# Adding the token stream to layer 0's mixed inputs: an accumulating DMA over both channel chunks in place of GpSimd's additions

## The chip, the cores and the metric

The kernel runs on one core of a Trainium2 chip. The metric is the device time of the whole program in microseconds; the figure quoted for the kernel before is the median of three runs. Five engines work side by side and meet through semaphores: TensorE (PE, with its weight loads shown as PEld), VectorE (DVE), ScalarE (ACT), GpSimd (POOL) and SyncE (SP). Transfers are issued from the queues of SP, ACT and POOL.

## The reference, cut to what matters

Two layers are computed on a stream of 8 x 512 tokens with 256 channels. In each layer the stream is normalised, a token mixer and a mixture of experts both read it, and both outputs are added to it. Layer 0's mixer is a bidirectional linear recurrence (RWKV style), its experts are 8 with the best 2 chosen; layer 1 has two attentions and 16 experts with a shared one.

The change lies in the front of layer 0's mixer, in the lines that make its five mixed inputs:

```
dx = xc - x                                  # xc: a 3-tap convolution along the tokens
xxx = x + dx * maa_x
t5 = tanh(xxx @ maa_w1).reshape(B, T, 5, 32)
m = einsum('btfc,fcd->fbtd', t5, maa_w2)
xw = x + dx * (maa_w + m[0])
xk = x + dx * (maa_k + m[1])
xv = x + dx * (maa_v + m[2])
xr = x + dx * (maa_r + m[3])
xg = x + dx * (maa_g + m[4])
r, k, v, g = xr @ Wr, xk @ Wk, xv @ Wv, silu(xg @ Wg)
w = time_decay + tanh(xw @ decay_w1) @ decay_w2
...
S = exp(wt)[..., None] * S + kt[..., None] * vt[..., None, :]    # the scan, forwards and backwards
```

The change is about who adds the leading `x` in the five lines from `xw` to `xg`.

## The kernel before, in words

**Layout.** A sequence (one of B = 8, index `b`) is kept transposed: channels on the 128 partitions, in NC = 2 chunks `c`, and T = 512 tokens along the row. `xnT` (L711) holds the normalised stream of one sequence with two columns of padding at each side; `xT[c]` are its inner 512 columns. There is one `xnT` buffer, so the next sequence's loading (the memsets L749 and L750 on GpSimd, the load L751 on SP) waits until the last reader of the present one is done.

**The order of the work.** The kernel is written as Python generators, each of which issues some instructions and then yields. `Turns.turn()` (L155) runs every live generator once; the order of the calls is the order of the instructions on PE, DVE, ACT and SP, whose order is pinned (L35, L373). GpSimd's order is not pinned: a scheduler sets it when the program is built. An engine works through its own list strictly in order.

In the main stage `scans` (L887) drives the turns. It goes through 128 units (b, c, vg), four turns each: a product of 128x1024 (L901), two scans forwards and backwards (L910, L914) in each of two turns, a second product (L923); PE sums the results two units later (L929). So one sequence is 64 turns. In each turn the other generators add a piece: `experts` (L592) works off 39 chunks of 256 token slots, 12 turns a chunk (L615 gate and up, L655 down); `ending` closes a chunk of channels; and `projections(b + 1)` (L672) prepares the next sequence while the present one is scanned.

`projections` has three generators, run one after the other for b >= 1 (L897): `inputs`, `values`, `decays`. For b = 0 they run beside the first normalisations (L1010 to L1018), before any scan, and `first` is true. Counting their yields gives 11 turns for `inputs`, 12 for `values` and 22 for `decays`: 45 of the 64.

**The lines of the change.** `mixed(*fs)` (L722) makes mixed inputs for the projections named by `fs`. It is called with (2, 1) in `values` for xv and xk, with (0, 3) in `decays` for xw and xr, and with (4) late in `decays` for xg. For each chunk `c` it issues the small matmuls on PE (L732, L734), yields, has VectorE write `(m + maa) * dx` (L739) and has GpSimd add `xT[c]` in place (L742). After both chunks it yields twice and returns the tiles, and the caller's matmuls come next (L697 for v, k, r and g; L815 for dw). One sequence has ten such additions, 128x512 fp32 each; eight sequences have 80.

The tiles come from `mix` (L688): tag `xf`, four buffers of 128x512. For b = 0 those of `decays` and the two `near` tiles take the `held` buffers instead.

**Other GpSimd work of the main stage.** It issues the experts' indirect gathers (L567 weights `wgu` and `wdn`, L577 tokens `xs`), stores the experts' results (L665), and multiplies `z` by `g` (L987), 16 times in all. `entry` (L273), which starts layer 1 on a sequence, gathers two expert rows per token into `y0` (L284 to L290) and adds them up (L298); in layer 0's last part `y0` and `cT` use the `xf` buffers as well (L1029).

Of the kernel before, what the change touches and what calls it, by code (L numbers as in the profile page):

```python
# [26 lines left out]
F32 = mybir.dt.float32  # L27
I32 = mybir.dt.int32
AF = mybir.ActivationFunctionType
ALU = mybir.AluOpType  # L30
# [6 lines left out]
P = 128  # L37
B, T, D = 8, 512, 256
NC = D // P
NT = T // P  # L40
H = 16
HD = 16
PAD = 2
# [122 lines left out]
def two_layers(ctx: ExitStack, tc: tile.TileContext, a: dict, out: bass.AP):  # L166
    nc = tc.nc
    vec_e, act_e, pool_e, pe = nc.vector, nc.scalar, nc.gpsimd, nc.tensor
# [8 lines left out]
    def held(i, shape, name):  # L177
        return hold.tile(shape, F32, tag=f"held{i}", name=name)
# [18 lines left out]
    def V(name, c):  # L197
        return vecs[:, VEC[name], c : c + 1]
# [9 lines left out]
    outs = stream.tile([NSLOT, D], F32, name="outs")  # L208
    slot = [const.tile([P, NTT], I32, name=f"slot{i}", tag=f"slot{i}") for i in range(2)]
# [63 lines left out]
    def entry(b):  # L273

        if b >= 3:
            yield from until("out", b - 3)
        bank, temp = place_of["bank"], place_of["temp"]
        acc = held(b % 3, [P, NT, D], f"acc{b}")
        nc.sync.dma_start(acc, tokens(after[b]))
        ahead = 2 if b else NT  # L280
        for t0 in range(0, NT, ahead):
            ys = []
            for t in range(t0, t0 + ahead):
                y = temp([P, 2, D], "y0", f"y0_{b}_{t}", ahead)  # L284
                n = b * NT + t
                for i in range(2):
                    pool_e.indirect_dma_start(
                        out=y[:, i, :], out_offset=None, in_=outs,
                        in_offset=bass.IndirectOffsetOnAxis(ap=slot[i][:, n : n + 1], axis=0),
                    )  # L290
                ys.append((t, n, y))
            yield
            yield
            if b == 0:
                yield from until("scans over")
            for t, n, y in ys:
                for i in range(2):
                    vec_e.scalar_tensor_tensor(  # L298
                        acc[:, t, :], y[:, i, :], wslot[i][:, n : n + 1], acc[:, t, :],
                        ALU.mult, ALU.add,  # L300
                    )
        yield
        x = held(3 + b % 3, [P, NT, D], f"x1_{b}")
        yield from layer_norm(x, acc, f"b{b}")
        yield
        if b >= 2:
            yield from until("ffn", b - 2)
        pss = transposed(bank, x, f"x_{b}")
        yield
        xT = held(6 + b % 2, [P, NC, T], f"xT_{b}")  # L310
        for c in range(NC):
            act_e.copy(xT[:, c, :], pss[c])
        own[b] = acc, x, xT
        done.add(("x", b))
        yield

        ps = bank(f"lg_{b}")
        for t in range(NT):
            for c in range(NC):
                pe.matmul(  # L320
                    ps[:, t * E1 : (t + 1) * E1], xT[:, c, t * P : (t + 1) * P], rtw[:, c, :],
                    start=c == 0, stop=c == NC - 1,
                )
        yield


        def rt(n, tag):
            return small.tile([P, NT, n], F32, tag=tag, name=f"{tag}_{b}", bufs=1)

        s, sb, sel = rt(E1, "rs"), rt(E1, "rsb"), rt(E1, "rsel")  # L330
        gsel, gs = rt(G1, "rg"), rt(G1, "rgs")
        act_e.activation(s.rearrange("p n e -> p (n e)"), ps[:, : NT * E1], AF.Tanh, scale=0.5)
        yield
        vec_e.tensor_scalar(s, s, 0.5, 0.5, ALU.mult, ALU.add)
        vec_e.tensor_tensor(sb, s, bc(cbias, 1, NT), ALU.add)

        def groups(x):
            return x.rearrange("p n (g e) -> p (n g) e", g=G1)

        chosen(groups(sel), groups(sb), E1 // G1, 2, C["tri4"], temp, f"g{b}")  # L340
        yield
        vec_e.tensor_tensor(sel, sel, sb, ALU.mult)
        vec_e.tensor_reduce(gs.rearrange("p n g -> p (n g)"), groups(sel), AX.X, ALU.add)
        chosen(gsel, gs, G1, 2, C["tri4"], temp, f"h{b}")
        flat = gsel.rearrange("p n g -> p (n g)")
        vec_e.tensor_tensor(groups(sb), groups(sb), bc(flat, 2, E1 // G1), ALU.mult)
        vec_e.tensor_scalar(gsel, gsel, FMAX, FMAX, ALU.mult, ALU.subtract)
        vec_e.tensor_tensor(groups(sb), groups(sb), bc(flat, 2, E1 // G1), ALU.add)
        for t in range(0, NT, 2):
            yield  # L350
            chosen(sel[:, t : t + 2, :], sb[:, t : t + 2, :], E1, 4, C["tri16"], temp, f"i{b}{t}")
        yield
        vec_e.tensor_tensor(sel, sel, s, ALU.mult)
        tot = small.tile([P, NT], F32, tag="rtot", name=f"rtot_{b}")
        vec_e.tensor_reduce(tot, sel, AX.X, ALU.add)
        vec_e.tensor_scalar(tot, tot, 1e-20, None, ALU.add)
        vec_e.reciprocal(tot, tot)
        vec_e.tensor_tensor(sel, sel, bc(tot, 2, E1), ALU.mult)
        yield
        ps = bank(f"cT_{b}")  # L360
        for t in range(NT):
            pe.transpose(ps[:E1, t * P : (t + 1) * P], sel[:, t, :], ident)
        yield
        cT = temp([E1, T], "cT", f"cT_{b}")
        act_e.copy(cT, ps[:E1, :])
        cd = shares_at.tile([E1, T], F32, tag="cd", name=f"cd_{b}")
        act_e.dma_start(cd, cT)
        own[b] += (cd,)
        done.add(("entry", b))


    with ExitStack() as l0:
        l0.enter_context(tc.manual_schedule(engines=PINNED))  # L373
        keep = l0.enter_context(tc.tile_pool(name="keep0", bufs=1))
        rw = l0.enter_context(tc.tile_pool(name="rw", bufs=1))
# [296 lines left out]
        def projections(b):  # L672


            first = b == 0
# [10 lines left out]
                return ps_gu.tile([P, T], F32, tag="gu", name=f"{name}_{b}") if first else bank(name)  # L686

            def mix(name, i, other=False):  # L688
                if other and first:
                    return held(i, [P, T], f"{name}_{b}")  # L690
                return rw.tile([P, T], F32, tag="xf", name=f"{name}_{b}", bufs=4)

            def project(w, xs, co, name, bank=bank):

# [16 lines left out]
            xnT = rw.tile([P, NC, T + 2 * PAD], F32, tag="xnT", name=f"xnT_{b}")  # L711
            xT = [xnT[:, c, PAD : PAD + T] for c in range(NC)]
            dx = big("dx", 1)
            dxs = [dx[:, c, :] for c in range(NC)]
            t5a = rw.tile([P, T], F32, tag="t5a", name=f"t5a_{b}")
            th = rw.tile([96, T], F32, tag="th", name=f"th_{b}")
# [4 lines left out]

            def mixed(*fs, other=False):  # L722

                xs = {f: [] for f in fs}
                for c in range(NC):
                    pss = []
                    for f in fs:
                        ps = (other_bank if other else bank)(f"m{f}{c}")
                        cols = slice(c * P, (c + 1) * P)
                        if f < 4:  # L730
                            rows = slice(32 * f, 32 * f + 32)
                            pe.matmul(ps, m2a[rows, cols], t5a[rows, :], start=True, stop=True)  # L732
                        else:
                            pe.matmul(ps, m2b[64:, cols], t5b, start=True, stop=True)  # L734
                        pss.append(ps)
                    yield
                    for f, ps in zip(fs, pss):
                        t = mix(f"xf{f}{c}", 2 * c + (f != fs[0]), other)
                        vec_e.scalar_tensor_tensor(  # L739
                            t, ps, V("maa_" + "wkvrg"[f], c), dxs[c], ALU.add, ALU.mult  # L740
                        )
                        pool_e.tensor_tensor(t, t, xT[c], ALU.add)  # L742
                        xs[f].append(t)
                yield
                yield
                return [xs[f] for f in fs]

            def inputs():
                pool_e.memset(xnT[:, :, 0:PAD], 0.0)  # L749
# [11 lines left out]
                    yield  # L761
                for _ in range(0 if first else 1):
                    yield
                xxx = []
                for c in range(NC):
                    t = mix(f"xxx{c}", c)
                    vec_e.scalar_tensor_tensor(t, dxs[c], V("maa_x", c), xT[c], ALU.mult, ALU.add)
                    xxx.append(t)
                for _ in range(1 if first else 2):
                    yield  # L770
                both = ((t5a, 0, 0, P), (t5b, P, 64, 96))
                pss = []
                for _, lo, r0, r1 in both:
                    ps = bank(f"t5{lo}")
# [32 lines left out]
            def decays():  # L807
# [5 lines left out]
                ps = other_bank("dw")  # L813
# [22 lines left out]
                vec_e.scalar_tensor_tensor(q, d, 1.0, q, ALU.add, ALU.mult)  # L836
                yield

                near = [mix(f"near{c}", 4 + c, True) for c in range(NC)]
                for c in range(NC):  # L840
                    act_e.activation(near[c], q[:, c, :T], AF.Ln, scale=-1.0)
                for c in range(NC):
# [177 lines left out]
        def begin():  # L1020
# [6 lines left out]
            act_e.dma_start(cbias, a["correction_bias"].to_broadcast([P, E1]))  # L1027

            tag_of = {  # L1029
                "y0": ("xf", 4), "gt4": ("t5a", 1), "eq4": ("th", 1), "gt16": ("dx", 1),  # L1030
                "eq16": ("xnT", 1), "cT": ("xf", 4),
            }
            place_of["bank"] = lambda name: ps_gu.tile([P, T], F32, tag="gu", name=name)
            place_of["temp"] = lambda shape, tag, name, bufs=1: rw.tile(
# [509 lines left out]
```

## Time and profile before

| What | Value |
|---|---|
| median of 3 runs | 2727.75 us (2727.06 to 2733.11) |
| the profiled execution | 2728.59 us, span 2726.8 us |
| PE, DVE busy | 2362.4 us (87%), 2157.0 us (79%) |
| ACT, POOL busy | 888.3 us (33%), 477.5 us (18%) |
| GpSimd's additions, L742 | 80 of 128x512, 113.3 us busy by the page |
| first scan product (L901) starts at | 97.9 us |
| last scan product (L923) starts at | 1422.5 us |

The span is the time of the profiled execution by its own records; the device time of that execution is 1.8 us longer. The page's second part cuts the span in 40 slices. Slices 3 to 21 are the main stage, in which DVE stands at 8 or 9 tenths throughout and PE mostly as well; the second half is layer 1, in which PE leads. In a group line the columns are the source line, the engine, the operation, output and inputs with shapes, the count, busy time and mean duration of one, and the idle time of the engine just before them with what ended it.

### The profile page before, as it was taken

The page shows a single profiled execution, that of the slowest core. Times are in us where ns is not written, and L with a number is a line of the kernel's source. Part 1 is how long each engine was busy: PE and PEld are TensorE (multiplying, and loading weights), DVE is VectorE, ACT ScalarE, POOL GpSimd, SP SyncE. Part 2 cuts the span into 40 slices and gives each one's busy share as a digit, 9 for nine tenths or more (in the row PEclk, how much of TensorE's full clock was granted, in tenths as well). Part 3 has the DMA queues.
Part 4 walks back from the last instruction along what each step waited for, and adds up shares of the span by engine and source line. Part 5 has one row for each costly group of instructions (what it writes and reads, how often), then busy time and mean ns, then how long its engine had stood idle before and what let it go on. Part 6 is the DMA issues. An engine that isn't in the chain of part 4 may idle for free.

```text
span 2726.8 us, 32763 instructions
## 1 busy us (share of the span) xinstructions
PE 2362.4 (87%) x11900; PEld 1412.8 (52%) x11900; DVE 2157.0 (79%) x3063; ACT 888.3 (33%) x1687; POOL 477.5 (18%) x441
## 2 busy tenths in 40 slices
PE   6699898988989889898826899999989989898996
PEld 4355555555556545555503445555555555555554
DVE  7799999899999989989985755656576675756666
ACT  1233232222323123231102334434333434434344
POOL 2132232322223223232012100010010101001000
PEclk9688998989889899999957899999989989998998
DMA  6335455455465544655443100000010111000000
GB/s 219 112 104 148 141 176 148 142 146 156 138 176 153 158 133 138 173 151 140 138 122 104 43 16 17 20 27 25 20 36 20 32 32 31 25 24 21 20 9 17
DMA packets 100832, 248.87 MB, mean 91 GB/s; under 512 B 24992, under 2 KB 50368, under 8 KB 95552
## 3 DMA queue, kind: packets, MB, share of 16 engines
q1 hardware_dynamic: 70528, 113.32, 15.0%
q0 software_dynamic: 21168, 115.75, 13.6%
q10 hardware_dynamic: 8976, 17.69, 1.8%
q8 instruction: 96, 1.57, 0.2%
q14 instruction: 64, 0.52, 0.1%
HBM read 215.22 MB, written 31.46 MB: 90 GB/s over the span
## 4 chain that ended last, share of the span: by engine, by line
PE 57%; DVE 25%; DMA 6%; issue 6%; ACT 2%; SPq 2%; POOL 1%; DVEq 0%; ACTq 0%; POOLq 0%
PE y L1427 6%; PE y L655 6%; PE g L1381 5%; DMA kv<-vd 5%; PE g L615 4%; PE u L1381 4%; PE u L615 4%; DVE kv L910 3%; PE sc_g L1279 2%; DVE kv L901 2%; PE ys L929 2%; PE o_g L1307 2%; DVE kv L914 2%; PE qkv_l L1171 2%; SPq L878 2%
## 5 line engine op out<-in xcount | busy, mean ns | idle before, releaser
L914 DVE TENSOR_TENSOR_SCAN kv<-d,kv 128x512 f32<-128x512 f32 x256 | 336.7, 1315 | 8.8
L655 PE MATMUL y<-wdn,h 128*128 128x256 f32 x936 | 286.6, 443 | 54.9 <-DVE h L624 50.5
L910 DVE TENSOR_TENSOR_SCAN kv<-dq,kv 128x512 f32<-128x512 f32 x256 | 320.0, 1250 | 3.4
L655 PEld LDWEIGHTS y<-wdn,h 128*128 128x128 f32 x936 | 180.6, 211 | 186.6 <-issue 83.5
L1287 ACT ACTIVATE pt_g<-sc_g 128x512 f32<-128x512 f32 (+1 forms) x384 | 171.2, 531 | 275.0 <-PE sc_g L1279 215.3
L615 PE MATMUL g<-xsT,wgu 128*128 128x256 f32 x936 | 229.2, 388 | 4.7 <-ACT h L639 3.2
L1381 PE MATMUL g<-xT,w 128*128 128x512 f32 x384 | 203.7, 656 | 25.9 <-DVE att_l L1335 14.0
L615 PEld LDWEIGHTS g<-xsT,wgu 128*128 128x128 f32 x936 | 176.1, 192 | 57.4 <-issue 27.4
L1381 PE MATMUL u<-xT,w 128*128 128x512 f32 x384 | 188.5, 614 | 10.7 <-ACT qkT_g L1239 6.0
L615 PE MATMUL u<-xsT,wgu 128*128 128x256 f32 x780 | 196.3, 392 | 0.0
L1427 PE MATMUL y<-w,h 128*128 128x256 f32 x768 | 183.6, 392 | 0.7 <-ACT qkT_g L1239 0.7
L901 DVE TENSOR_TENSOR kv<-kv,k 128x1024 f32<-128x1024 f32 x128 | 172.0, 1344 | 6.6 <-DMA kv<-vd 6.6
L615 PEld LDWEIGHTS u<-xsT,wgu 128*128 128x128 f32 x780 | 149.5, 195 | 51.4 <-issue 22.8
L923 DVE TENSOR_TENSOR kv<-kv,r 128x1024 f32<-128x1024 f32 x128 | 162.9, 1273 | 3.6
L929 PE MATMUL ys<-kv,cst 128*32 128x512 f32 x512 | 105.7, 701 | 65.4 <-DVE kv L923 65.1
L1399 DVE TENSOR_TENSOR h<-h,u 128x512 f32<-128x512 f32 x96 | 66.0, 688 | 121.5 <-PE u L1381 116.6
L1427 PEld LDWEIGHTS y<-w,h 128*128 128x128 f32 x768 | 144.4, 193 | 34.2 <-issue 11.2
L639 ACT ACTIVATE h<-g 128x512 f32<-128x512 f32 (+1 forms) x117 | 61.7, 527 | 272.6 <-PE g L615 262.5
L1293 DVE TENSOR_TENSOR pt_g<-pt_g,cst 128x512 f32<-128x512 f32 x128 | 85.2, 686 | 75.1 <-ACT pt_g L1287 75.1
L742 POOL TENSOR_TENSOR xf<-xf,xnT 128x512 f32<-128x512 f32 x80 | 113.3, 1436 | 124.1 <-DVE xf L739 123.8
L1381 PEld LDWEIGHTS g<-xT,w 128*128 128x128 f32 x384 | 72.6, 201 | 110.7 <-issue 84.8
L1287 ACT ACTIVATE pt_l<-sc_l 128x384 f32<-128x384 f32 (+1 forms) x256 | 98.0, 469 | 86.3 <-PE sc_l L1279 70.7
(307 smaller groups left out, 3874.5 us busy)
## 6 DMA issues: line engine op xcount, KB each, us to landing
kv<-vd SPq DMA_DIRECT2D x1024, 64.0 KB
cb<-cd SPq DMA_DIRECT2D x128, 128.0 KB
outs<-ys POOLq DMA_DIRECT2D x39, 256.0 KB
w<-in_w ACTq DMA_DIRECT2D x12, 384.0 KB
xn<-in_x SPq DMA_DIRECT2D x8, 512.0 KB
xnT<-xT ACTq DMA_DIRECT2D x16, 256.0 KB
normed<-xn SPq DMA_DIRECT2D x8, 512.0 KB
xnT<-xnT SPq DMA_DIRECT2D x8, 512.0 KB
```

Of the source, the lines that this page charges most:

```text
L615: pe.matmul(o, w[:, at + c * P : at + (c + 1) * P], xT[:, c, :], start=c == 0, stop=c == NC - 1,)
L655: pe.matmul(y[:, n, :], hs[j // 2][lo:, j % 2, n * P : (n + 1) * P], wd[lo:, j * D : (j + 1) * D], start=j == 0, stop=j == NJ0,)
L742: pool_e.tensor_tensor(t, t, xT[c], ALU.add)
L901: vec_e.tensor_tensor(kv, kv, bc(kc, 1, NV), ALU.mult)
L910: vec_e.tensor_tensor_scan(out=kv[:, i, :], data0=qc, data1=kv[:, i, :], initial=0.0, op0=ALU.mult, op1=ALU.add,)
L914: vec_e.tensor_tensor_scan(out=kv[:, i, ::-1], data0=dc[:, ::-1], data1=kv[:, i, ::-1], initial=0.0, op0=ALU.mult, op1=ALU.add,)
L923: vec_e.tensor_tensor(kv, kv, bc(rc, 1, NV), ALU.mult)
L929: pe.matmul(y[r0 : r0 + 32, :], C["take"][:, 24 - 8 * at : 56 - 8 * at], kv[:, i, :], start=at == 0, stop=at == 3, skip_group_check=True,)
L1287: act_e.activation(pt[:, i, :end], scs[i][:, :end], AF.Exp, scale=0.25)
L1293: vec_e.tensor_tensor(pt[:, :, a0 : a0 + m], pt[:, :, a0 : a0 + m], bc(mask[:, :m], 1, 4), ALU.mult,)
L1381: pe.matmul(ps, w[:, k, c * P : (c + 1) * P], xT[:, c, :], start=c == 0, stop=c == NC - 1,)
L1427: pe.matmul(y[:, i, :], hs[k][:, (t + i) * P : (t + i + 1) * P], w1[j - 5 + k][:, 2, :], start=k == 0, stop=k == 5,)
```

## The change

GpSimd's addition after each VectorE instruction goes. The two chunks of a mixed input now share one tile [128, 2, 512], and when VectorE has written both, GpSimd issues one DMA that adds `xnT`'s inner columns (both chunks, 512 KB) into the tile. `mixed` then yields three times for b = 0 and four times otherwise, where it yielded twice. Per sequence there are five such DMAs, 40 in all.

The tag `xf` becomes two buffers of 128x2x512 in place of four of 128x512. Everything that shares the tag follows: `xxx` and `near` become one tile with two halves, `y0` holds the rows of two token tiles in one tile (`ahead // 2` buffers in place of `ahead`), and the bookkeeping for `cT` and `y0` names two buffers.

```diff
@@ entry @@
-            for t in range(t0, t0 + ahead):
-                y = temp([P, 2, D], "y0", f"y0_{b}_{t}", ahead)
-                n = b * NT + t
-                for i in range(2):
...
+            for t in range(t0, t0 + ahead, 2):
+                y = temp([P, 2, 2, D], "y0", f"y0_{b}_{t}", ahead // 2)
+                for j in range(2):
+                    n = b * NT + t + j
+                    for i in range(2):
...
@@ mix @@
                 if other and first:
-                    return held(i, [P, T], f"{name}_{b}")
-                return rw.tile([P, T], F32, tag="xf", name=f"{name}_{b}", bufs=4)
+                    return held(i, [P, NC, T], f"{name}_{b}")
+                return rw.tile([P, NC, T], F32, tag="xf", name=f"{name}_{b}", bufs=2)
@@ mixed @@
-                xs = {f: [] for f in fs}
+                xs = [mix(f"xf{f}", i, other) for i, f in enumerate(fs)]
                 for c in range(NC):
...
                     yield
-                    for f, ps in zip(fs, pss):
-                        t = mix(f"xf{f}{c}", 2 * c + (f != fs[0]), other)
+                    for f, x, ps in zip(fs, xs, pss):
                         vec_e.scalar_tensor_tensor(
-                            t, ps, V("maa_" + "wkvrg"[f], c), dxs[c], ALU.add, ALU.mult
+                            x[:, c, :], ps, V("maa_" + "wkvrg"[f], c), dxs[c], ALU.add, ALU.mult
                         )
-                        pool_e.tensor_tensor(t, t, xT[c], ALU.add)
-                        xs[f].append(t)
-                yield
-                yield
-                return [xs[f] for f in fs]
+                for x in xs:
+                    pool_e.dma_start(x, xnT[:, :, PAD : PAD + T], accum_op=ALU.add)
+                for _ in range(3 if first else 4):
+                    yield
+                return [[x[:, c, :] for c in range(NC)] for x in xs]
@@ inputs, decays @@
-                    t = mix(f"xxx{c}", c)
...
+                both = mix("xxx", 0)
+                xxx = [both[:, c, :] for c in range(NC)]
...
-                near = [mix(f"near{c}", 4 + c, True) for c in range(NC)]
+                both = mix("near", 4, True)
+                near = [both[:, c, :] for c in range(NC)]
@@ begin @@
-                "y0": ("xf", 4), "gt4": ("t5a", 1), "eq4": ("th", 1), "gt16": ("dx", 1),
-                "eq16": ("xnT", 1), "cT": ("xf", 4),
+                "y0": ("xf", 2), "gt4": ("t5a", 1), "eq4": ("th", 1), "gt16": ("dx", 1),
+                "eq16": ("xnT", 1), "cT": ("xf", 2),
```

More of the change, by code (lines that the diff above doesn't have):

```diff
@@ L282, in entry @@
             ys = []
-            for t in range(t0, t0 + ahead):
-                y = temp([P, 2, D], "y0", f"y0_{b}_{t}", ahead)
-                n = b * NT + t
-                for i in range(2):
[L287 to L291, printed above, removed]
+            for t in range(t0, t0 + ahead, 2):
[3 more added lines that the diff above has]
+                    for i in range(2):
+                        pool_e.indirect_dma_start(
+                            out=y[:, j, i, :], out_offset=None, in_=outs,
+                            in_offset=bass.IndirectOffsetOnAxis(ap=slot[i][:, n : n + 1], axis=0),
+                        )
+                    ys.append((t + j, n, y[:, j]))
             yield
@@ L763, in inputs @@
                     yield
-                xxx = []
+                both = mix("xxx", 0)
+                xxx = [both[:, c, :] for c in range(NC)]
                 for c in range(NC):
-                    t = mix(f"xxx{c}", c)
-                    vec_e.scalar_tensor_tensor(t, dxs[c], V("maa_x", c), xT[c], ALU.mult, ALU.add)
-                    xxx.append(t)
+                    vec_e.scalar_tensor_tensor(
+                        xxx[c], dxs[c], V("maa_x", c), xT[c], ALU.mult, ALU.add
+                    )
                 for _ in range(1 if first else 2):
```

## The prediction

> **What bounds the kernel now.** I read the busy table and the slices first, then stretches of time, then the durations of single instructions, then GpSimd's and VectorE's timelines side by side, then the waits.
>
> ```profile
> span 2726.8 us, 32763 instructions
> PE 2362.4 (87%) x11900; PEld 1412.8 (52%) x11900; DVE 2157.0 (79%) x3063; ACT 888.3 (33%) x1687; POOL 477.5 (18%) x441
> PE   6699898988989889898826899999989989898996
> DVE  7799999899999989989985755656576675756666
> ```
>
> The main stage (slices 3 to 21, from 97.9 us to about 1424 us) is close to bound by DVE, with PE right behind it. I cut one sequence (b = 3) into quarters of 16 turns:
>
> ```profile
> 618.60:661.60 43.00, 35.66 (x135) 20.24 (x131) 42.15 (x48) 11.31 (x17) 13.11 (x12) 0.96 0.51 153
> 661.60:705.30 43.70, 43.38 (x165) 26.26 (x164) 36.82 (x37) 10.45 (x17) 14.89 (x13) 1.00 0.54 164
> 705.30:752.40 47.10, 42.33 (x144) 26.03 (x144) 44.63 (x47) 19.38 (x27) 8.74 (x9) 0.78 0.39 111
> 752.40:784.80 32.40, 27.95 (x117) 19.02 (x116) 31.70 (x31) 4.48 (x9) 11.10 (x9) 0.91 0.76 219
> ```
>
> The columns are the stretch, its length, busy PE, PEld, DVE, ACT and POOL, then clock, DMA share and GB/s. DVE is the limit in the first, third and fourth quarter (42.15 of 43.00, 44.63 of 47.10, 31.70 of 32.40), PE in the second (43.38 of 43.70): that is where v, k, dw and r are projected.
>
> Next, GpSimd beside DVE at two places:
>
> ```profile
> L914 DVE TENSOR_TENSOR_SCAN kv<-d,kv x256: 1224/1224/2214, 101.0 to 1421.2; 128x512 f32<-128x512 f32 x128
> L901 DVE TENSOR_TENSOR kv<-kv,k x128: 1210/1219/3799, 97.9 to 1416.4; 128x1024 f32<-128x1024 f32 x128
> ```
>
> ```profile
> 324.99 5.21 POOL L742 TENSOR_TENSOR xf<-xf,xnT 128x512 f32<-128x512 f32 x4
> 349.50 3.06 POOL L742 TENSOR_TENSOR xf<-xf,xnT 128x512 f32<-128x512 f32 x2 [3.83 <-DVE xf L739]
> ```
>
> ```profile
> 325.46 3.80 DVE L901 TENSOR_TENSOR kv<-kv,k 128x1024 f32<-128x1024 f32 x1
> 349.99 1.68 DVE L910 TENSOR_TENSOR_SCAN kv<-dq,kv 128x512 f32<-128x512 f32 x1
> 351.70 1.93 DVE L914 TENSOR_TENSOR_SCAN kv<-d,kv 128x512 f32<-128x512 f32 x1
> ```
>
> A product that takes 1.22 us takes 3.80 us while four additions run, and a scan of 1.22 us takes 1.68 or 1.93 us beside two. Wherever GpSimd adds, DVE is slow; so part of "DVE busy" is DVE being held up.
>
> **What the Trainium skill says.** "SBUF — State Buffer", section "Who interferes with whom": a DVE instruction with two SBUF inputs contends with a GpSimd instruction that reads SBUF, and the one that comes second is blocked; DMA has ports of its own. The trace agrees on the first (1.22 us to 3.80 us above). On the second: the DVE instructions that overlap only GpSimd's DMA issues (394 of them) are together 0.2 us shorter than usual, so issuing costs DVE nothing. "DMA: Bandwidth & Descriptors", section "SWDGE vs HWDGE vs iDMA": a DMA that accumulates can be issued from GpSimd only, and GpSimd has one queue; the page shows just one software queue (q0, 115.75 MB), which the experts' gathers use too. Same page, "Rules for kernel authors": an accumulating DMA reads its destination and writes it later. No run here shows one yet.
>
> **The change part by part.**
>
> *Removed: 80 additions.* What they cost DVE, from means and medians: L914 has mean 1315 against 1224, times 256 = 23.3 us; L910 1250 against 1219, times 256 = 7.9 us; L901 1344 against 1219, times 128 = 16.0 us; L923 1273 against 1224, times 128 = 6.3 us. That is 53.5 us. Splitting it instruction by instruction by what overlaps gives 45.7 us for L742 (the rest of some 11 us is L987, the product of z and g, which stays). Of the 45.7 us, 2.3 us lie before the first scan and 43.4 us in the main stage: 4.2 us in first quarters, 28.0 us in second, 11.2 us in third ones, summed over b = 0 to 6.
> In third quarters, and mostly in first ones, DVE is the limit (95 to 98% busy), so I count 0.9 of 15.4 us: 14 us. In second quarters PE is at 92 to 99%, and taking time from DVE alone gives little. But the two extra turns in each `mixed` also move projection matmuls out of these quarters into the third, where PE has room (84 to 90%), and a held-up DVE makes PE wait too (PE waits 65.1 us for L923 and 50.5 us for L624). Bounds 0 and 28 us; I take three quarters, since both engines gain slack when no single instruction is stretched to 3.8 us: 21 us. Sum of the gain: 35 us.
>
> *Added: 40 accumulating DMAs of 512 KB.* The issue is about 0.8 us of GpSimd (L665, 256 rows too: 0.762 us) against two additions of 1.1 to 2.1 us: GpSimd gets freer. Landing: the store L665 (256 KB) has its data moving for 1.7 us (median), and a lone gather's first packet starts 1.7 us after its issue begins. For 512 KB the data needs 3.5 us at L665's rate, and at most double if reading the destination costs as much again: first landing 5.5 to 9 us after the issue, the second of a pair 9 to 16 us. The skill's price for a plain DMA ("DMA: Bandwidth & Descriptors", "Anatomy of one DMA", 2.0 us + bytes / 436e3 per us) gives 3.2 us, an estimate below my lower end. I take 6.5 and 10.5 us.
>
> The cover is the time from the last L739 to the consumer, plus the two added turns. A turn is 2.5 us (160 us a sequence by 64); on PE alone an experts' piece (eight L615) is 1.73 us. So two turns are 3.5 to 5 us, say 4.5. From the trace of before, b = 2 to 6:
> - v comes 7.2 to 9.1 us after L739, with two turns 12 to 13.5 us: covered, and k lies later still. Cost 0; without cover 3 us a sequence.
> - dw comes 0.5 to 2.6 us after, with two turns 5 to 7 us, against 6.5: a stall of about 1 us. r comes a turn later, 8 to 9.5 us against 10.5: about 1.5 us. PE waits with the experts' matmuls (L615, L655) queued behind, and DVE waits for those through L624. 2.5 us x 7, of which 0.7 counts since PE is the limit there: 12 us. Bounds: 0 (plain copy rate) and 8 us x 7.
> - g comes 0 to 7 us after; 1 us more of stall x 7, in a quarter where PE has 10% to spare: 0.2 of it, 1 us.
>
> *Queues.* The accumulating DMA stands in q0 behind a weight gather (issue to last byte 8.0 us for wgu, 5.7 for wdn, medians) if one is in flight. In the built order the DMAs of (0, 3) come after wdn and the store where they came before, and those of (4) mostly after wgu and two xs; since their VectorE writes lie two and four turns later as well, these gathers are largely through. The memset for the next `xnT` now waits for the last DMA and holds GpSimd's list for some 6 us; behind it stand gathers that wait for PE anyway (POOL waits 341 us for L655 before wdn). The load of `xnT` on SP is needed 20 turns later. I count 0 to 8 us, taken as 1. DMA share (0.39 to 0.76) grows by 40 x 2 to 4 us in 1325, 6 to 12 points; DVE waited 6.6 us for kv in all: 1 us.
>
> *Turns.* Projections take 51 of 64 turns in place of 45, so scans never wait for them: 0. Before the first scan, one turn more with the same data waits: -2 to +6 us, taken as +1.
>
> *Tiles.* `xf`, `xxx`, `near`: same bytes, same readers: 0. `y0`: in layer 1 the third token tile's gather waits for the fourth L298 in place of the second, 2 x 0.484 us a sequence. DVE is not the limit there (458 of 700 us busy from 2000 us on, PE 634). 0 to 7 us, taken as 1.
>
> Sum: -35 + 12 (dw, r) + 1 (g) + 1 (queues) + 1 (DMA share) + 1 (start) + 1 (`y0`) = -18 us against the profiled 2728.6 us (span 2726.8 plus 1.8 around it): 2710.6. That execution is 0.8 us above the median of the runs, so 2710.
>
> **The rivals.**
> - *Full relief.* The DMAs land in time and second quarters give all they hold: 45.7 us less, 1 us lost: 2683. For: the same quarters without additions, b = 7, run at 33.0 and 34.5 us; against: PE there has no projections either.
> - *PE takes it all.* Second quarters give nothing, and 12 us of stalls with the small items cancel the 14 us of the others: within 4 us of 2728. For: 43.38 of 43.70.
> - *Slower: the landing outlasts the turns.* At 9 and 16 us after the issue, dw stalls PE for 3 us, r for another 5, g for 4. At a weight of 0.8 in second quarters and 0.4 in third ones that is 8 us a sequence, 56 in all; with 4 us of the small items and 35 gained, +25: 2753. For: nothing shows the rate of an accumulating DMA, and gathers may stand ahead of it in q0; against: two added turns. It decides once stalls pass 31 us, or 4.4 us of counted stall a sequence: when the first of a pair lands later than about 8 us after its issue.
>
> That the change does not do what it says is no rival: the 80 additions are gone from the built program.
>
> **How the numbers follow.** Forecast 2710 with chance 0.50; full relief 0.17; PE takes it all 0.12; slower 0.21. Faster by over 0.2% (5.5 us, about what a measurement of this kernel can tell from no change) are the first two, 0.67. The range runs from 2678, full relief with some 5 us for calmer turns, to 2752, just short of the slower case's middle: half of that case and little else is left out.
>
> **What would show it.** DVE's L914 and L901 should have means of 1.23 to 1.25 us (L987 stays) and DVE's busy time in all falls by some 45 us. PE's wait for the accumulating DMA before L815 and L697 should total 10 to 30 us; over 60 us means the slower case. Second quarters shrink by 2 to 4 us, third by 1 to 2. I am wrong if those waits are long, if second quarters don't shrink though DVE is freed, or if the time is lost in layer 1.

## The result, and the profile after

The changed kernel takes 2719.3 us (median of 8 runs, 2713.9 to 2723.8) against 2727.7 us of the kernel before: a ratio of 0.9965, with a 95% interval of 0.9955 to 0.9975. By the ratio, which is estimated from all the runs, it is faster by about 9.5 us (0.0035 of 2727.7); the two medians lie 8.3 us apart. The forecast was 18 us, so the direction and the range held, and the gain is half of what was forecast. The profiled execution took 2723.8 us, 4.4 us more than the median and the longest of the eight.

The head of its page: span, busy times, VectorE's slices, and the software queue that carries the new DMAs.

```profile
span 2722.0 us, 32771 instructions
PE 2354.2 (86%) x11900; PEld 1418.0 (52%) x11900; DVE 2116.6 (78%) x3063; ACT 883.2 (32%) x1683; POOL 413.7 (15%) x401
DVE  7799999798999978999975755656566775756666
q0 software_dynamic: 32048, 136.73, 17.9%
```

VectorE's slices 3 to 21 stand at 7 to 9 tenths, where they stood at 8 or 9, and the software queue now carries 136.73 MB (115.75 before). VectorE has 40.4 us less to do, by its busy time, with the same 3063 instructions: none was removed from it. But the main stage became only about 9 us shorter (99 to 1416 us against 98 to 1424), so VectorE, busy for 94.5% of it before, is busy for 92.1% now. It has become faster, and waits more. The four groups of the scan show where the 40.4 us come from (the last figures of a line are busy time, mean ns of one, and idle time before, in us but for the mean):

```profile
L917 DVE TENSOR_TENSOR_SCAN kv<-d,kv 128x512 f32<-128x512 f32 x256 | 324.2, 1267 | 8.8
L913 DVE TENSOR_TENSOR_SCAN kv<-dq,kv 128x512 f32<-128x512 f32 x256 | 311.2, 1216 | 3.7
L904 DVE TENSOR_TENSOR kv<-kv,k 128x1024 f32<-128x1024 f32 x128 | 155.9, 1218 | 12.3 <-DMA w<-in_w 6.6
L926 DVE TENSOR_TENSOR kv<-kv,r 128x1024 f32<-128x1024 f32 x128 | 156.9, 1226 | 3.4
```

The products of L904 (L901 before) had a mean of 1344 ns and a longest of 3799; now the mean is 1218 and the longest 1226. That part of the argument is plain in the profile: the additions had stretched VectorE's instructions.

What came in return is in PE's waits of the main stage, 99 to 1420 us (total, times, longest):

```profile
PE y L656 <- DVE h L625: 47.6, 22, 5.1
PE ys L932 <- DVE kv L926: 46.7, 14, 14.1
PE m L736 <- DVE xf L740: 35.1, 7, 7.6
...
PE v L699 <- DMA xf<-xnT: 6.2, 3, 2.7
...
PE g L699 <- DMA xf<-xnT: 3.9, 1, 3.9
PE dw L817 <- DMA xf<-xnT: 3.5, 3, 1.8
...
PE r L699 <- DMA xf<-xnT: 0.9, 2, 0.7
```

The waits for the new DMAs are short: 14.5 us on PE, with the weight loads 31.3 us. The third line is new and larger than all of them. It has nothing to do with the DMA: the small matmuls `m` of xg wait for VectorE's L740. PE's timeline at one of the seven places:

```profile
729.58 1.12 PE L736 MATMUL m<-th,m2b 32*128 32x512 f32 x2
730.63 0.66 PE L985 MATMUL rs<-cst,wide 128*128 128x128 f32 x4
731.12 1.89 PE L616 MATMUL g<-xsT,wgu 128*128 128x256 f32 x8
738.59 2.07 PE L736 MATMUL m<-th,m2b 32*128 32x512 f32 x2 [5.58 <-DVE xf L740]
```

`m` and the transpose `rs` take turns in the same two PSUM buffers. The four added turns in front of `mixed(4)` put an `rs` between the `m` of chunk 0 and that of chunk 1. So chunk 1 needs the buffer that chunk 0's `m` holds, and PE, whose list is fixed, stands for 5.6 us until VectorE has read it.

In quarters, as in the prediction, summed over b = 0 to 6 (one profiled execution of each kernel, us): the first went from 341.8 to 335.1, the second from 301.6 to 283.4, the third from 319.1 to 334.4, the fourth from 226.8 to 225.5. The second quarters gave what was forecast, and the third took most of it back.

### The profile page after: what moved, and what is told of

Its sections match the earlier page's. It is cut to its first block, busy times and chain, and to the rows that moved or that the text cites. A ratio compares the mean times of both kernels' runs of the same rounds, so it can differ in the third digit from the quotient of the medians.

```text
span 2722.0 us, 32771 instructions
## 1 busy us (share of the span) xinstructions
PE 2354.2 (86%) x11900; PEld 1418.0 (52%) x11900; DVE 2116.6 (78%) x3063; ACT 883.2 (32%) x1683; POOL 413.7 (15%) x401
## 3 DMA queue, kind: packets, MB, share of 16 engines
q0 software_dynamic: 32048, 136.73, 17.9%
## 4 chain that ended last, share of the span: by engine, by line
PE 54%; DVE 21%; issue 10%; DMA 9%; SPq 2%; ACT 2%; POOL 2%; ACTq 0%; DVEq 0%; POOLq 0%
PE y L1430 6%; PE y L656 5%; PE g L1384 5%; PE u L1384 4%; DMA kv<-vd 4%; PE g L616 4%; PE u L616 3%; DMA xf<-xnT 2%; PE sc_g L1282 2%; SPq L881 2%; DVE kv L913 2%; PE o_g L1310 2%; PE ys L932 2%; DVE kv L917 2%; PE qkv_l L1174 2%
## 5 line engine op out<-in xcount | busy, mean ns | idle before, releaser
L917 DVE TENSOR_TENSOR_SCAN kv<-d,kv 128x512 f32<-128x512 f32 x256 | 324.2, 1267 | 8.8
L656 PE MATMUL y<-wdn,h 128*128 128x256 f32 x936 | 280.9, 438 | 49.8 <-DVE h L625 47.6
L913 DVE TENSOR_TENSOR_SCAN kv<-dq,kv 128x512 f32<-128x512 f32 x256 | 311.2, 1216 | 3.7
L656 PEld LDWEIGHTS y<-wdn,h 128*128 128x128 f32 x936 | 180.4, 210 | 174.1 <-issue 83.3
L904 DVE TENSOR_TENSOR kv<-kv,k 128x1024 f32<-128x1024 f32 x128 | 155.9, 1218 | 12.3 <-DMA w<-in_w 6.6
L1430 PEld LDWEIGHTS y<-w,h 128*128 128x128 f32 x768 | 144.4, 194 | 34.2 <-issue 11.2
L926 DVE TENSOR_TENSOR kv<-kv,r 128x1024 f32<-128x1024 f32 x128 | 156.9, 1226 | 3.4
L932 PE MATMUL ys<-kv,cst 128*32 128x512 f32 x512 | 95.6, 660 | 51.0 <-DVE kv L926 46.7
L1296 DVE TENSOR_TENSOR pt_l<-pt_l,cst 128x768 f32<-128x768 f32 (+1 forms) x128 | 107.9, 886 | 12.7 <-ACT pt_l L1290 12.7
```

What stands on the lines that cost most here:

```text
L656: pe.matmul(y[:, n, :], hs[j // 2][lo:, j % 2, n * P : (n + 1) * P], wd[lo:, j * D : (j + 1) * D], start=j == 0, stop=j == NJ0,)
L904: vec_e.tensor_tensor(kv, kv, bc(kc, 1, NV), ALU.mult)
L913: vec_e.tensor_tensor_scan(out=kv[:, i, :], data0=qc, data1=kv[:, i, :], initial=0.0, op0=ALU.mult, op1=ALU.add,)
L917: vec_e.tensor_tensor_scan(out=kv[:, i, ::-1], data0=dc[:, ::-1], data1=kv[:, i, ::-1], initial=0.0, op0=ALU.mult, op1=ALU.add,)
L926: vec_e.tensor_tensor(kv, kv, bc(rc, 1, NV), ALU.mult)
L932: pe.matmul(y[r0 : r0 + 32, :], C["take"][:, 24 - 8 * at : 56 - 8 * at], kv[:, i, :], start=at == 0, stop=at == 3, skip_group_check=True,)
```

## The experiments

The theories at the start: (A) the additions' contention was worth about what was forecast, and the bank of `m` gives it back; (B) the landing of the DMAs gives it back; (C) something else that came with the change does. All ratios are to the kernel before, with 95% intervals; it was timed again beside each group of experiments. "us" below are medians. Sums over quarters come from one profiled execution each.

### Turns, tiles, additions and DMAs one by one

*Turns only.* The kernel before, with the change's turns and its additions kept:

```diff
-                yield
-                yield
+                for _ in range(3 if first else 4):
+                    yield
```

> The kernel before with only the yields of the change (3 for b = 0, otherwise 4, in place of 2); GpSimd still adds. Bank theory (the four turns bring the matmuls of xg onto the `rs` transposes of `ending`, so that the second of them, m41, finds its PSUM bank taken until VectorE has read m40): third quarters grow by 10 to 15 us in sum and PE waits some 30 us for L739 before L734; in all +5 to +14 us, 2733 to 2742. DMA theory (the gain was eaten by the landing and the traffic of the accumulating DMAs): no loss without them, second quarters a little shorter, 2720 to 2728.

Measured: 2731.0 us, 1.0008 (0.9999 to 1.0017). The time lies between the two expectations. The wait is there without any DMA; the second quarters lost 9.3 us and the third ones gained 13.4 us in length:

```profile
PE m L734 <- DVE xf L739: 35.1, 7, 7.7
```

So the bank wait belongs to the turns.

*Tiles only.* The new tiles, with the additions and the two turns of before:

```diff
-                for x in xs:
-                    pool_e.dma_start(x, xnT[:, :, PAD : PAD + T], accum_op=ALU.add)
-                for _ in range(3 if first else 4):
-                    yield
+                        pool_e.tensor_tensor(x[:, c, :], x[:, c, :], xT[c], ALU.add)
+                yield
+                yield
```

> The changed kernel's tiles (two buffers of double width, `y0` in one tile) with GpSimd's additions and two turns as before: no more than 3 us from the kernel before by every theory, 2724 to 2731; if `y0` costs what the prediction bounded, up to 7 us more behind the last scan.

Measured: 2728.9 us, 1.0000 (0.9992 to 1.0009). The tiles, `y0` among them, cost nothing, as every theory had it.

*Neither additions nor DMAs, with two turns, and with four:*

```diff
-                for x in xs:
-                    pool_e.dma_start(x, xnT[:, :, PAD : PAD + T], accum_op=ALU.add)
-                for _ in range(3 if first else 4):
-                    yield
+                yield
+                yield
```

(With four turns only the two DMA lines go.) Both kernels leave the stream out of the five mixed inputs, so they serve for timing alone.

> The changed kernel's tiles without the accumulating DMAs and with two turns after each mixed input, as in the kernel before; the stream is left out of the five mixed inputs. If the parts add up (additions gone -28 us, DMAs +16, turns +4 by the runs so far): 2697 to 2703, some 4 us below the run with four turns. If the added turns help once the additions are gone, because projection matmuls then leave the second quarters: 2705 to 2712, second quarters longer than the 269 us of four turns by 8 us or more.

> The changed kernel without the accumulating DMAs (the stream is left out of the five mixed inputs), turns as changed. Bank theory: third quarters stay within 4 us of the changed kernel's 327 us; only PE's 14 us of waits for the DMA go, 2712 to 2718. DMA theory: third quarters fall back to about 310 us and the time to 2695 to 2705.

Measured: 2696.7 us, 0.9887 (0.9872 to 0.9902) with two turns; 2703.1 us, 0.9918 (0.9905 to 0.9932) with four. The intervals lie just apart: once the additions are gone, the turns alone cost 0.0031, or 8.5 us. With two turns the parts added up as expected, to within 1 us. With four the time is the one that the DMA theory named, but the third quarters stayed at 330.1 us and didn't fall back to 310, as the bank theory had it.

*The DMAs with two turns:*

```diff
-                for _ in range(3 if first else 4):
-                    yield
+                yield
+                yield
```

> The changed kernel with two turns in place of three or four, so that only the cover goes. If the DMA's price is its landing, which the turns hide: PE waits for the DMA grow from 14 us to 50 us or more, above all before dw and g, whose cover falls to 0 to 3 us against 5 us of landing; 2740 to 2785. If the price is the traffic or GpSimd's queue: 2714 to 2724.

Measured: 2815.4 us, 1.0312 (1.0298 to 1.0326). PE's waits, 97 to 1510 us:

```profile
PE g L699 <- DMA xf<-xnT: 61.4, 8, 11.6
...
PE dw L817 <- DMA xf<-xnT: 25.3, 7, 5.7
...
PE v L699 <- DMA xf<-xnT: 14.2, 3, 5.7
```

That is beyond even the 2785 us that was expected at most. Without cover the DMAs cost 119 us over the kernel that has none. The two added turns are no ornament: with them the kernel is 96 us faster, though by themselves they cost 8. Lost cover is not all of it: the DMA for xg is issued 0.3 us after VectorE's last write in the changed kernel, but here 2.7 to 4.5 us after it in five of the eight sequences, behind a gather in GpSimd's list. The next experiments show the same.

The parts together, in ratios: additions away -0.0113 (two turns), turns +0.0031, DMAs +0.0047 (0.9965 less 0.9918). In us of 2727.7: -30.8 + 8.5 + 12.8 = -9.5. The split depends on the order of the steps. With the turns first, they cost 0.0008 (2 us), and taking the additions away then gives 0.0090 (24.5 us).

### Is it the bank?

Two ways to move xg's `m` off the `rs`: three turns more in front of `mixed(4)`, or two turns fewer after `mixed(2, 1)`.

```diff
+                for _ in range(0 if first else 3):
+                    yield
                 (xg,) = yield from mixed(4)
```

> The changed kernel with three more turns ahead of the call for xg (b >= 1), which puts both its matmuls behind the `rs` transposes and VectorE's reading of them. Bank theory: PE's wait for L740 before L736 falls from 35 us to under 10, third and fourth quarters together fall by 10 us or more, 2704 to 2711. DMA theory: the same DMAs, the same traffic: 2716 to 2722.

```diff
-                for _ in range(3 if first else 4):
+                for _ in range(3 if first else 2 if fs[0] == 2 else 4):
```

> The changed kernel with two turns in place of four after xv and xk, so that the matmuls of xg come two turns earlier, both ahead of the `rs` transposes. Bank theory: 2703 to 2711, as the other way round; v had 7 us or more of cover already and the first DMA of a pair lands 5 us after its issue, so PE waits for v grow by less than 10 us in all. DMA theory: less cover and the same traffic, 2719 to 2728.

Measured: 2740.0 us, 1.0046 (1.0032 to 1.0060), and 2748.6 us, 1.0072 (1.0058 to 1.0085). Both are slower than the changed kernel, which neither theory had expected. The wait of L736 for L740 is gone in both, but each shift brought others, so these two runs don't show what the bank alone is worth. In the late one `g` met the landing:

```profile
PE g L699 <- DMA xf<-xnT: 41.6, 8, 11.1
```

and the fourth quarters grew by 28.5 us (225.5 to 254.0). GpSimd's list says why. VectorE's write of xg was done at 407.50 us there:

```profile
410.26 1.53 POOL L568 DMA_INDIRECT wdn<-in_w_dn,wrow  x1 [7.56 <-PE y L656]
411.79 0.77 POOL L666 DMA_DIRECT2D outs<-ys  x1
412.56 1.32 POOL L744 DMA_DIRECT2D xf<-xnT  x1
```

In four of the seven sequences the DMA stood behind a weight gather that itself waited for PE. It was issued 4.9 to 5.1 us after VectorE's write in place of 0.3, and its last byte landed 14.2 to 14.4 us after the write in place of 5.1 to 6.6. The shift had moved GpSimd's work as well, whose order isn't pinned. In the early one `var` and `rs` met occupied buffers, and `dw` and `v` lost cover:

```profile
PE var L968 <- ACT sq L960: 15.4, 5, 4.0
PE dw L817 <- DMA xf<-xnT: 13.7, 5, 3.4
...
PE rs L985 <- DVE xf L740: 11.3, 6, 2.5
PE v L699 <- DMA xf<-xnT: 11.2, 2, 5.6
```

To see the bank without a landing, the late shift was put on the kernel with no DMAs:

> As the run without DMAs and with four turns, with three more turns ahead of the call for xg: the PSUM bank without any landing in play. Bank theory: PE's wait for L740 (35 us) goes, third and fourth quarters together fall by 8 us or more, 2688 to 2696. If that wait only shows slack that PE has in third quarters: within 3 us of 2703.

Measured: 2699.8 us, 0.9895 (0.9880 to 0.9911), against 0.9918 (0.9905 to 0.9932): 6 us by the ratios, 3 us by the medians, with intervals that overlap, and between the two expectations. Third and fourth quarters are 8.5 us shorter in the profiled executions, but the one of this run is the fastest of its four, 7 us below their median. Nor is the bank quite free: `m` now waits 12.8 us there for VectorE's reading of `rs`. So the bank may be most of the turns' 8.5 us, which isn't shown, and it is not the 35 us of its wait.

### Is it the landing, or the traffic?

*Traffic only.* No additions, two turns, and 30 of the 40 DMAs made into spare tiles that nobody reads (again without the stream in the mixed inputs):

```diff
+                if b >= 2:
+                    ...
+                    for s, x in zip(spare, xs):
+                        vec_e.tensor_copy(s[:, 0, 0:1], x[:, 1, 0:1])
+                        pool_e.dma_start(s, xnT[:, :, PAD : PAD + T], accum_op=ALU.add)
```

> The run without additions and with two turns, and with the accumulating DMAs of b = 2 to 7 (30 of the 40) issued as in the changed kernel, after VectorE has written both chunks, but into two spare tiles that nobody reads (one VectorE copy of 128x1 ahead of each, to hold its place). The stream is left out of the mixed inputs. Landing theory (the DMA costs only what PE waits for it): 2696 to 2701, no more than 4 us above the run without DMAs. Traffic or queue theory (they slow the gathers, the kv spreads or VectorE): 0.75 of the 16 us that the DMAs cost with four turns, 2706 to 2712.

Measured: 2711.3 us (2703.1 to 2717.5), 0.9946 (0.9931 to 0.9962): on the side of the traffic, 16 us over the same kernel without them (0.9887). PE waits for none of these DMAs. What the trace shows is that the memset for the next `xnT` stood on GpSimd for them, and that VectorE waited twice, 14.3 us in all, for a load of `kv` (6.6 us, once, in the kernel before):

```profile
POOL xnT L756 <- DMA spare<-xnT: 28.8, 5, 9.5
```

The profiled execution, 2703.1 us, is the fastest of its six, 7 us above that of the kernel without DMAs, so it shows only about half of the cost. And part of the cost may be the run's own: it adds 30 small copies on VectorE and two memsets of the spare tiles, of which one held GpSimd's list for 19.2 us.

*One DMA of 256 KB per chunk*, each issued as soon as VectorE has written its chunk, with four turns and with three:

```diff
-                for x in xs:
-                    pool_e.dma_start(x, xnT[:, :, PAD : PAD + T], accum_op=ALU.add)
+                        pool_e.dma_start(x[:, c, :], xT[c], accum_op=ALU.add)
```

> The changed kernel with one accumulating DMA of 256 KB per chunk, the first chunk's a turn earlier (80 DMAs, same bytes). Landing theory: what PE waits for is half as long on its way, its waits for the DMA fall from 14 us (and 17 before the weight loads) to under half; 2706 to 2715. Queue theory: twice the issues and completions, 2720 to 2728.

> As the one per chunk, with three turns in place of four for every sequence. Landing theory: a turn less of cover (2.5 us) against 1.5 to 3 us of shorter landing, so about as much waiting as in the changed kernel, and 2 to 3 us less for the turns: 2712 to 2722. If the waits come back in full as with two turns: over 2740.

Measured with four turns: 2703.1 us, **0.9916** (0.9900 to 0.9932). That is less than either theory expected. It beats both kernels, and equals the kernel with no DMAs at all (0.9918), though every byte is moved. The bank wait is still there, the waits for DMAs are nearly gone (94 to 1393 us):

```profile
PE m L736 <- DVE xf L740: 35.1, 7, 7.6
...
PE v L699 <- DMA xf<-xnT: 1.7, 2, 1.5
...
PE g L699 <- DMA xf<-xnT: 1.6, 1, 1.6
...
PE dw L816 <- DMA xf<-xnT: 0.4, 1, 0.4
```

With three turns: 2759.0 us, 1.0122 (1.0105 to 1.0140), some 40 us above what the landing theory expected. As in the early shift, `dw` lost its cover and `var` met an occupied buffer (27.2 and 15.4 us), and the third quarters grew to 368.5 us.

*Both pieces late.* The first piece above is smaller and also a turn earlier. To part the two:

```diff
                 for x in xs:
-                    pool_e.dma_start(x, xnT[:, :, PAD : PAD + T], accum_op=ALU.add)
+                    for c in range(NC):
+                        pool_e.dma_start(x[:, c, :], xT[c], accum_op=ALU.add)
```

> The changed kernel with two DMAs of 256 KB for each mixed input, one for each chunk, both issued where the one DMA of 512 KB was issued (after the second chunk); four turns as before. It parts the two differences of the run with a DMA for each chunk (2703 us, ratio 0.9916): the first chunk's DMA there is both smaller and a turn earlier. If the earlier issue is what mattered, the last bytes land no sooner here than with one DMA, and this run stays near the changed kernel, 2714 to 2722 us. If the smaller piece mattered (the projection's matmuls of a chunk wait only for that chunk, and others' transfers get between the pieces), this run is near 2703, at most 2708 us. GpSimd issues ten DMAs a sequence at about 1 us in both kernels, so its own time doesn't part them.

Measured: 2708.0 us, 0.9928 (0.9914 to 0.9942). That is within what was expected of the smaller piece, but the run can't tell, because the new lines didn't move the pieces. GpSimd's order is set by the scheduler, and GpSimd and VectorE at b = 2 show what it made of this kernel:

```profile
487.02 1.86 POOL L745 DMA_DIRECT2D xf<-xnT  x2 [6.77 <-DVE xf L740]
490.25 1.05 POOL L568 DMA_INDIRECT wgu<-in_w_gu,wrow  x1 [1.37 <-PE u L616]
491.27 1.89 POOL L745 DMA_DIRECT2D xf<-xnT  x2
```

```profile
485.96 1.41 DVE L740 SCALAR_TENSOR_TENSOR xf<-m,vecs,dx 128x512 f32<-128x512 f32 x2 [4.64 <-PE m L734]
489.02 1.41 DVE L740 SCALAR_TENSOR_TENSOR xf<-m,vecs,dx 128x512 f32<-128x512 f32 x2
```

Two DMAs are issued before VectorE begins to write the second chunk: they are the first chunk of v and that of k, and they follow their own write, as in the run before. In the traces of the two runs the order of work is the same on every engine, and each of the 80 pieces follows its write at the same distance, within 0.02 us. So this is a second measurement of one program, and 0.9916 and 0.9928 show how far two such measurements fall apart. Together they say that pieces issued when each is ready gain 0.0037 to 0.0049 over one DMA. Whether the smaller size or the earlier issue does it stays open.

*Where the pieces gain.* The second quarters sum to 270.3 us with pieces (the second of the two measurements), like those of the kernel without DMAs (269.3), against 283.4 with one DMA. Nearly all of these 13 us lie in three sequences: b = 2 (45.6 against 40.4), b = 3 (42.6 against 38.4) and b = 5 (44.1 against 40.4).

PE's timeline at b = 2, first in the kernel with one DMA, then in the one with pieces:

```profile
492.85 3.05 PE L656 MATMUL y<-wdn,h 128*128 128x256 f32 x12
498.39 3.78 PE L699 MATMUL v<-xf,wmix 128*128 128x512 f32 x4 [2.49 <-DMA xf<-xnT]
501.97 2.76 PE L656 MATMUL y<-wdn,h 128*128 128x256 f32 x6
```

```profile
495.40 3.05 PE L656 MATMUL y<-wdn,h 128*128 128x256 f32 x12
498.38 1.12 PE L699 MATMUL v<-xf,wmix 128*128 128x512 f32 x2
499.76 1.13 PE L699 MATMUL v<-xf,wmix 128*128 128x512 f32 x2 [0.25 <-DMA xf<-xnT]
500.72 1.46 PE L656 MATMUL y<-wdn,h 128*128 128x256 f32 x6
```

A wait of 2.49 us became one of 0.25. But look at the work after it: four `v` matmuls take 3.78 us in one and 1.12 + 1.13 in the other, six L656 take 2.76 and 1.46. The windows of the kernel with one DMA say why (length, busy PE, PEld, DVE, ACT, POOL, then the granted clock, DMA share and GB/s):

```profile
493.80:497.80 4.00, 2.10 (x9) 1.24 (x7) 3.93 (x4) 0.00 (x0) 0.66 (x1) 1.00 1.00 212
497.80:504.60 6.80, 6.21 (x11) 3.61 (x12) 6.66 (x6) 0.59 (x1) 0.00 (x0) 0.50 0.93 237
504.60:508.60 4.00, 4.00 (x14) 2.27 (x13) 1.90 (x3) 1.17 (x2) 0.39 (x1) 1.00 0.29 91
```

With the wait TensorE's clock fell to half for 6.8 us, which costs PE 3.4 us of work on top of the 2.5. At b = 5 the same is seen, a wait of 2.69 us for `v` and half clock from its last part on. At b = 3 the clock is at half from 651.4 to 665.0 us with only a 0.8 us gap ahead of it; that one isn't explained by a wait for a DMA, and in the late shift above, with the same single DMAs, this quarter takes 38.3 us. So the 4.2 us of b = 3 are not the price of the larger DMA. Summed over b = 0 to 6, second quarters have 21.9 us of half clock with one DMA, all of it in these three sequences, and 5.9 with pieces: 16.0 us, worth 8.0 us of PE's work, and the waits make up most of the rest of the 13. This counts only where PE is the limit: without DMAs 9.6 us of half clock fall in the second quarter of b = 0, which is no longer for it (34.2 us against 34.0).

Why that DMA was late there: the first packets of a lone one move 1.9 us after its issue begins, and the last byte has landed at 4.8 us. The pair at b = 2 was issued behind an experts' weight gather:

```profile
487.70 0.99 POOL L568 DMA_INDIRECT wgu<-in_w_gu,wrow  x1 [11.70 <-PE u L616]
488.68 2.60 POOL L744 DMA_DIRECT2D xf<-xnT  x2
```

In the one software queue the pair's first packets moved 5.5 and 7.9 us after their issue began, and the last bytes had landed at 8.9 and 11.9 us; at b = 5 at 8.8 and 12.1. With pieces the first chunks of v and k went ahead of the gather and had landed 3.2 and 4.1 us after their issue (b = 5: 3.1 and 3.9). The second chunks stood behind it as before (7.6 and 9.1 us). But `v` could begin with its first chunk, and waited 0.25 us for the second.

## Why the forecast was half right

*Removed additions: right, a little high.* Forecast 35 us, measured 30.8 (0.9887, two turns), or 24.5 after the turns. The second quarters gave 20.2 us (301.6 to 281.4) where 21 were taken; the first and third gave 9.7 where 14 were taken. The match in the second quarters is in part luck. Of the two reasons given for 21 us, one was the added turns, and the 20.2 came without them. Such sums are rough, too: the kernel with the new tiles alone has 307.5 us there, at the same total time as the kernel before. VectorE's busy time fell by 40.4 us (forecast some 45). The means fell to 1216 to 1226 ns except for L917: 1267, where 1230 to 1250 were forecast. Its excess over the 1224 ns of an undisturbed one is 11 us in all, as much as the prediction had put down to the product of z and g, which stays; nearly all of it (10.6 us) falls on 13 scans that run beside that product.

*Turns: 0. This is the step that failed.* The prediction counted only that the projections still fit in 64 turns. But a turn also moves PE's small matmuls past others that share their buffers. Four turns put xg's `m` onto `rs`, with 35.1 us of PE waits that two turns don't have, and the turns as a whole cost 8.5 us once the additions are gone. How much of this the bank is stays open: moving `m` away without DMAs gave back some 3 to 6 us, within the noise. The third quarters, said to shrink by 1 to 2 us each, grew by 2.2.

The forecast's sum against the measured one: 18, less 4.2 for the additions, less 8.5 for the turns, with 2.2 back from the DMAs and 2 for the start and `y0`, which this split doesn't count apart, leaves 9.5.

*The DMAs: the size right, the working only in part.* Forecast 15 us, 12 of it for `dw` and `r`; measured 12.8, with four turns. DMA's share of the main stage rose by 9 points (0.50 to 0.59), inside the 6 to 12 forecast. The waits total 14.5 us on PE, inside the forecast's 10 to 30. But they fell on `v` most (6.2 us), which the prediction called covered, and less on `dw` (3.5) and `r` (0.9). Landing was quicker than taken: 4.8 to 7.0 us for the first of a pair (6.5 taken) and 6.8 to 9.5 for the second (10.5), but for the two pairs behind a gather. The prediction looked for gathers ahead of the DMAs of (0, 3) and (4), and not of (2, 1), where they were, at b = 2 and b = 5. There `v` was also wanted 8.0 us after VectorE's write, not 12 to 13.5, and its DMA landed 9.7 us after it. That the total came out near the forecast is therefore partly luck. And the wait isn't the whole price: the half clock after it was left out, though the Trainium skill has it ("TensorE: Matmul & The Clock Gate", section "Why this matters for your kernels": no idle gaps over some 3 us between bursts of matmuls, or the clock falls to half). The trace agrees, and is stricter. I counted PE's gaps that begin at full clock in the main stages of seven executions (before, after, without DMAs at two and at four turns, one DMA at two turns, and both with pieces at four), from the trace's clock records. Of those of 2.5 us or more, 136 of 141 are followed by half clock that sets in by 3.5 us after their end, of those of 2.0 to 2.5 us 33 of 47, of those of 0.5 to 1.0 us 30 of 134. A stretch at half clock lasts 6.8 us in the median.

The rival "landing outlasts the turns" named the right point: with two turns the DMAs cost 119 us, and with pieces, each issued when its chunk is ready, nothing that can be measured (0.9916 and 0.9928 against 0.9918).

*What stays open.* DMAs that nobody reads cost 16 us with two turns, more than those that are read cost with four. So part of the changed kernel's 12.8 us may be the burst of 512 KB itself and GpSimd's held memset, not the landing, or the 16 us may be in part what that run adds. That pieces of 256 KB with the same bytes cost nothing speaks against the bytes and for the size of a burst, its place in the queue or its earlier start, but unread pieces weren't tried. Nor was a kernel with GpSimd's order pinned, which could part these three. Also untried is the version with pieces and with `m` off the `rs` bank.

## What to carry to other kernels

Where two engines contend, look for the stretched durations on the engine that is the limit; what they lose is the gain, here 30.8 us by one order of the steps and 24.5 by the other, where 35 were forecast. Work that is handed to a DMA has to land under cover: smaller pieces, issued when each is ready, shorten the landing and cost nothing here, while added turns in a fixed order of instructions are a new schedule, whose buffers and banks have to be looked through one by one. Where a scheduler sets an engine's order, a change in the source can move more than it says, or nothing at all: compare the issue times in the trace with the writes that they follow before a run is read as a test. And a wait of TensorE of 2.5 us or more (2.0 to 2.5 us in most cases here) is to be priced with the stretch at half clock behind it.

## What the runs showed of the hardware

- GpSimd's additions of two SBUF operands stretched VectorE's products from 1.22 to as much as 3.80 us; with DMAs in their place the longest is 1.226 us.
- An accumulating DMA within SBUF moves a packet of 2048 bytes in 0.182 us (median), a packet of that size on the hardware queues takes 0.084 us. 512 KB are 256 such packets, 16 for each of the 16 DMA engines: 2.9 us by estimate. In the changed kernel they landed 4.7 to 12.1 us after the issue began (median 6.3), 256 KB, with four turns, after 3.0 to 9.7 us (median 4.5). The issue took 1.33 us of GpSimd (median) for 512 KB and 0.99 for 256 KB, where the prediction took 0.8.
- GpSimd's list holds a DMA back behind a gather that waits for PE, though the DMA's own data is ready: xg's DMA was issued 4.9 to 5.1 us after VectorE's write in four sequences of the late shift, 0.3 us after it in the changed kernel.
- The number of turns doesn't act in one direction: with pieces, four turns gave 0.9916 and 0.9928 and three 1.0122; with one DMA, two gave 1.0312, four 0.9965, and three more before xg 1.0046.
